# Attention in groups of four key slots, with one exponential over two PSUM banks

## The chip, the cores and the metric

The kernel runs on one core of one Trainium2 chip. The time is device microseconds of one launch, the median of several runs. Engines are named as in the profile: PE (TensorE matmuls), PEld (its weight loads), DVE (VectorE), ACT (ScalarE), POOL (GpSimd) and SP (SyncE, which issues all DMAs here).

## The reference

A block of three residual steps on x of shape (4, 1024, 128), in float32:

```python
x = x + 0.5 * ffn(layernorm(x))              # 8 experts, dense, weighted by a router
x = x + attn(layernorm(x))                   # attn has its own layernorm, and adds its input
x = x + 0.5 * ffn(layernorm(x))

# attn: 16 heads of 64, latents of 64
c_q, c_kv = h @ w_down_q.T, h @ w_down_kv.T
q, k, v = heads(c_q @ w_up_q.T), heads(c_kv @ w_up_k.T), heads(c_kv @ w_up_v.T)
q, k = rope(q), rope(k)
attn = softmax(q @ k.T / sqrt(64))           # no mask, 1024 keys
out = merge(attn @ v) @ w_out.T + residual
```

## The kernel before

The kernel has three stages one after another on all engines: the first feed-forward part (`ffn`), attention (the loop over `g` in `run`), the second feed-forward part (`ffn2`). The order of instructions on each engine is the order in which the program issues them; it is written by hand. The change is in attention.

**Units and slots.** Heads are taken in pairs `P` (32 of them: 4 batches by 8), queries in halves of 512. A pair and a half is a unit `U` (64 of them). In a unit, the 1024 keys are eight chunks of 128; one chunk is a slot `s` (512 in all). For a slot, `score` (L689) multiplies keys by queries for both heads of the pair (`hh`), in four accumulating steps `k`: three products of split high and low parts, and one that subtracts the row maximum (`one_row` by `maxr`). The two heads use the two row halves of the PE array side by side, tiling 64\*128 in the profile. An exponential (L705) turns the scores into `p`. POOL sums the `p` of slots 0 to 6 in `acc` (L717). `values` (L719) multiplies `p` by the latent (`psc`, L724; both heads beside each other by columns, 128\*64). After a unit, `den` (L728) sums `p` and `acc` over keys with ones, and the sum goes through DRAM to become a column `dT`; `outp` (L751) multiplies the unit's output by the folded matrix `G`, and DVE scales it by the reciprocal and adds it to `X` (L766).

**Maxima.** `passA` (L665) runs 15 slots ahead (`AHEAD`): one pair of matmuls into the two banks `psA`, and a DVE maximum over both (L677). `psA` is not doubled, so a pair must wait until the maximum before it has been taken. After eight of them `max_row` sends the maxima through DRAM to `maxr`.

**Other work.** `rope` makes the queries and keys of later heads, one tile per unit: matmuls `mm` (L595), four DVE products (L583), two POOL combinations `e` and `o`, ACT casts `hi0` and `hi1`, a POOL subtraction `lo`, and two DMAs `dhi` and `dlo`. The generators in `streams` (norms, latents, router of the second feed-forward part) advance by one stage at each `step`. `at(g, fn)` puts work off to a later group, `run_later` does it. `loads` brings queries and keys of a pair back from DRAM.

**Banks.** PSUM has eight banks: two `psA`, four `psS` for scores, `psC` for values, `psX`. A slot's scores take `psS[2 * (s % 2) + hh]`. Between scores, `psX` and `psS[0]` serve `rope` and `outp`, `psS[1]` and `psS[2]` the streams (`aux`), and `psX` the denominator.

**The cycle.** A group `g` is two slots:

```python
passA; scores of slot 2g; [rope e0, adds of outp, step]; scores of slot 2g+1; passA
rope (mm, ...); run_later (outp, ...); step; den; rope (casts, lo)
values of the two slots of the group before
```

Projection, output and denominator each come once in four groups, in different ones.

Of the kernel before, what the change touches and what calls it, by code (L numbers as in the profile page):

```python
# [9 lines left out]
F32 = mybir.dt.float32  # L10
# [16 lines left out]
AHEAD = 15  # L27
NSLOT = B * 128
NGRP = NSLOT // 2
# [8 lines left out]
class Kernel:  # L38
# [10 lines left out]
    def setup(self):  # L49
# [7 lines left out]
        bank = lambda name, n=1: pool(name, 1, space=PSUM).tile([128, 512] if n == 1 else [128, n, 512], F32, name=name)  # L57
        self.psA, self.psS, self.psC, self.psX = bank("ps_a", 2), [bank(f"ps_s{i}") for i in range(4)], bank("psc"), bank("psx")
# [40 lines left out]
        self.ckn = [const.tile([128, TPB, 64], F32, name=f"ckn{i}") for i in range(2)]  # L99

# [53 lines left out]
    def ffn_weights2(self, wg, wu, wd):  # L154
        self.wg, self.wu, self.wd = (w.rearrange("p k (e i) -> p k e i", e=E) for w in (wg, wu, wd))
        for n, w in enumerate((self.wg, self.wu)):
            self.dma(out=w, in_=self.w_scr[n])
        self.dma(out=self.wd[:, 1], in_=self.wd_scr)
        for n in range(4):
            es = bass.ds(2 * n, 2)  # L160
            hi, lo = self.wd[:, 0, es], self.wd[:, 1, es]
            self.at(self.group + 4 + n, lambda hi=hi, lo=lo: self.nc.scalar.copy(hi, self.f(lo)))
            self.at(self.group + 5 + n, lambda hi=hi, lo=lo: self.nc.gpsimd.tensor_tensor(lo, self.f(lo), self.f(hi), ALU.subtract))
# [407 lines left out]
    def rope(self, n, stage):  # L571


        nc, P = self.nc, self.prep
        w = self.rope_of.setdefault(n, {})
        b, m = divmod(n, 16)
        g, qk, h = m // 4, m // 2 % 2, m % 2
        scr = (self.k_scr if qk else self.q_scr)[b][g]
        cs = slice(512 * h, 512 * h + 512)

        def half(eo, k):
            w[eo, k] = P.tile([128, 512], F32, name=f"rt{eo}{k}", tag=f"t{2 * eo + k}")
            nc.vector.tensor_tensor(w[eo, k], w["ps"][eo], (self.cos, self.sin)[k][:, cs], ALU.mult)  # L583

        if stage == "fetch":
            assert (b, qk, h) in self.latents
            w["C"] = P.tile([128, 2, 512], F32R, name="C_l", bufs=2)
            self.dma(out=w["C"], in_=self.c_scr[b][h][:, qk])
        elif stage == "mm":
            ps = w["ps"] = self.rope_banks  # L590
            hi, lo = w["C"][:, 0, :], w["C"][:, 1, :]
            for k, (wt, c) in enumerate(((self.wup1, hi), (self.wup1, lo), (self.wup2, hi))):
                for eo in range(2):
                    r64 = slice(64 * eo, 64 * eo + 64)
                    nc.tensor.matmul(ps[eo], wt[r64, qk * 4 + g, :], c[r64, :], start=k == 0, stop=k == 2)  # L595
            half(1, 0)
            half(1, 1)
        elif stage in ("e0", "e1"):
            half(0, int(stage[1]))
        elif stage == "e":  # L600
            w["eo"] = P.tile([128, 2, 512], F32, name="eo", bufs=2)
            nc.gpsimd.tensor_tensor(w["eo"][:, 0, :], w[0, 0], w[1, 1], ALU.subtract)  # L602
        elif stage == "o":
            nc.gpsimd.tensor_tensor(w["eo"][:, 1, :], w[0, 1], w[1, 0], ALU.add)  # L604
        elif stage in ("hi0", "hi1"):
            k = int(stage[2])
            if k == 0:
                w["hi"] = P.tile([128, 2, 512], F32R, name="hi_r")
            nc.scalar.copy(w["hi"][:, k, :], w["eo"][:, k, :])  # L609
        elif stage == "dhi":  # L610
            self.dma(out=scr[0:2, :, :, cs].rearrange("s h i t -> (h i) s t"), in_=w["hi"])
        elif stage == "lo":
            nc.gpsimd.tensor_tensor(w["eo"].bitcast(F32R), w["eo"], self.f(w["hi"]), ALU.subtract)  # L613
        elif stage == "dlo":
            self.dma(out=scr[2:4, :, :, cs].rearrange("s h i t -> (h i) s t"), in_=w["eo"])
            self.roped.add((b, g, qk, h))
            del self.rope_of[n]

    def attn_first(self):

        yield from self.attn_pre(0)
        steps = {-5: "fetch", 0: "mm e0 e1", 2: "e", 3: "o", 5: "hi0", 6: "hi1", 7: "dhi", 8: "lo", 10: "dlo"}
# [33 lines left out]
    def at(self, g, fn):  # L656

        self.later.setdefault(g, []).append(fn)

    def run_later(self, g):  # L660
        self.group, self.slot = g, 2 * g
        for fn in self.later.pop(g, []):
            fn()

    def passA(self, a):  # L665
# [12 lines left out]
        if i == 7:  # L678
            m = self.ms.tile([128, 8], F32R, name="m8")
            nc.vector.tensor_reduce(m, self.m_of.pop(U).rearrange("p h q k -> p (h q) k"), AX.X, ALU.max, negate=True)  # L680
            self.at(self.group, lambda: self.max_row(U, m))

    def max_row(self, U, m):
# [3 lines left out]
        self.at(self.group + 2, lambda: self.dma(out=self.maxr[U % 2][0:128:64, :].rearrange("h (q p) -> h q p", p=128), in_=d.rearrange("p (h q) -> h q p", h=2)))  # L687

    def score(self, s, hh, k):  # L689
# [9 lines left out]
        ps = self.psS[2 * (s % 2) + hh]  # L699
        w, x = ((K[r, 0, ks], Q[r, 0, qs]), (K[r, 0, ks], Q[r, 1, qs]), (K[r, 1, ks], Q[r, 0, qs]), (self.one_row[r, :], self.maxr[U % 2][r, :]))[k]  # L700
        nc.tensor.matmul(ps, w, x, start=k == 0, stop=k == 3)  # L701
        if k == 3:
            if hh == 0:
                self.p_of[s] = self.pp.tile([128, 2, 512], F32, name="p")
            nc.scalar.activation(self.p_of[s][:, hh, :], ps, AF.Exp, scale=0.125)  # L705
            if hh == 1:
                self.accumulate(s)
# [20 lines left out]
    def den(self, U):  # L728
# [3 lines left out]
        pd = self.psX  # L732
# [10 lines left out]
        self.at(self.group + 1, lambda: nc.sync.dma_start(out=dT, in_=d1.rearrange("(h x) (y p) -> p (h x y)", x=2, p=128)))  # L743
        self.at(self.group + 2, lambda: self.invert(U, osb, dT))

    def invert(self, U, osb, dT):
        rT = self.ms.tile([128, 8], F32, name="rT")
        self.nc.vector.reciprocal(rT, dT)
        self.at(self.group + 1, lambda: self.outp(U, osb, rT))

    def outp(self, U, osb, rT):  # L751
# [11 lines left out]
        def add(hh):  # L763
            for i in range(4):
                x = self.X[:, b * TPB + 4 * half + i, :]
                nc.vector.scalar_tensor_tensor(x, po[hh][:, i * 128:(i + 1) * 128], rT[:, 4 * hh + i:4 * hh + i + 1], x, ALU.mult, ALU.add)  # L766

        add(1)
        if self.bankO:
            self.mid.append(lambda: add(0))  # L770
        else:
            add(0)

    def run(self):
# [21 lines left out]
        with ExitStack() as ctx:  # L796
# [20 lines left out]
            def bg1(n, point):  # L817
# [9 lines left out]
                if point == 2 and n >= 64 - AHEAD:  # L827
                    self.group = (n - 64) // 2
                    self.passA(n - 64 + AHEAD)
                    if n % 2:  # L830
                        self.run_later(self.group)
# [36 lines left out]
        self.rest, self.rope_banks, self.bankO = self.psS[1:3], [self.psX, self.psS[0]], [self.psX, self.psS[0]]  # L868
        self.mid = []
# [25 lines left out]
        MID, TAIL, END = {1: "e0"}, {3: "hi0 hi1 lo"}, {-2: "fetch", 0: "mm", 1: "e1", 2: "e o", 4: "dhi", 5: "dlo"}  # L895

        def rope(g, table):
            for d, stages in table.items():
                n, r = divmod(g - d - 1, 4)
                if r == 0 and 0 <= n + NROPE < 16 * B and n >= 0:  # L900
# [3 lines left out]
        rope(-1, {-2: "fetch"})  # L904
        for g in range(NGRP + 1):
            s0 = 2 * g
            self.group, self.slot = g, s0

            for s in range(s0, min(s0 + 2, NSLOT)):
                if s == s0 and s + AHEAD < NSLOT:  # L910
                    self.passA(s + AHEAD)
                for k in range(4):
                    for hh in range(2):
                        self.score(s, hh, k)
                if s == s0:
                    rope(g, MID)
                    if self.mid:
                        self.mid.pop()()
                    if g % 2:
                        step(False)  # L920
                elif s + AHEAD < NSLOT:
                    self.passA(s + AHEAD)

            while self.mid:
                self.mid.pop()()
            self.nrest = 0
# [3 lines left out]
            rope(g, END)  # L930
            self.run_later(g)
            if g % 4 != 1:
                step(g % 4 != 3)
            if g == 2:
                for n, fn in enumerate(self.loads(2)):
                    self.at(g + 1 + n // 4, fn)
            if g < NGRP and g % 8 == 7:
                P = g // 8
                if P + 3 < NP:
                    for n, fn in enumerate(self.loads(P + 3)):  # L940
                        self.at(g + 1 + n // 4, fn)
                if P == NP - 2:
# [3 lines left out]
            if g and g % 4 == 0:  # L946
                self.den(g // 4 - 1)
            rope(g, TAIL)
            for s in range(s0 - 2, s0):
# [9 lines left out]
        with ExitStack() as ctx:  # L959
            self.ready, self.routed = set(range(6)), set(range(6))  # L960
            assert not (streams[1] or streams[2])
# [5 lines left out]
            def bg2(n):  # L967
                self.run_later(NGRP + 1 + n)
# [5 lines left out]
            self.ffn2(x_of, bg2, self.out.rearrange("(n p) d -> p n d", p=128))  # L974
        att.close()
# [54 lines left out]
```

## Time and profile before

| | us |
|---|---|
| median of 3 runs | 1777.81 (1777.41 to 1781.66) |
| profiled execution | 1775.35 |
| its span | 1773.6 |
| PE busy | 1677.1 |
| POOL busy | 1462.2 |
| DVE busy | 1302.2 |
| ACT busy | 912.4 |

The profile is of one execution. A row of the groups gives line, engine, operation, tiles and shapes, count, busy time, mean ns of one, and the idle time of the engine just before with what ended it. The timeline gives start, length, engine, line and count. Weight loads overlap matmuls, and matmuls overlap each other: a pair of row-tiled matmuls of 512 columns has a length of 0.39 us in the timeline but the next pair starts 0.23 us later, so starts are read, not lengths. The idle time of an engine that does not set the end costs nothing.

### The profile page before, as it was taken

Reading aid. Unit: us, or ns where it says so; the run is one execution under the profiler, and the core shown is the slowest. Engines: PE = TensorE matmul, PEld = TensorE weight load, DVE = VectorE, ACT = ScalarE, POOL = GpSimd, SP = SyncE. Lnnn points to the kernel's source line nnn. Section 1 sums busy time; section 2 is a strip of 40 time slices with the busy share of each in tenths; the row PEclk is TensorE's granted clock in tenths of the full one; section 3 lists DMA queues with packets and bytes.
Section 4 is the critical chain, followed back from the end, with each engine's and each line's share of the span. In section 5 each row is a group of like instructions: output and inputs, shape, how many; then the busy total and the mean of one; then the engine's idle time right before and its main releaser. Section 6 shows DMA issues by size and latency. Waiting matters only on the chain.

```text
span 1773.6 us, 31244 instructions
## 1 busy us (share of the span) xinstructions
PE 1677.1 (95%) x11428; PEld 1006.7 (57%) x11428; DVE 1302.2 (73%) x2223; ACT 912.4 (51%) x1916; POOL 1462.2 (82%) x803
## 2 busy tenths in 40 slices
PE   6898989999899999999999999999999999999998
PEld 5777755555455555555555555555555555456777
DVE  6676658777877778777787777687677766834887
ACT  4666655545455454554544455544544544445554
POOL 4448779899899998998998899898999987667666
PEclk9999999999999999999999999999999999999999
DMA  6025455455444444455444544544455442023443
GB/s 200 1 72 181 132 147 147 134 143 139 113 135 139 135 136 116 120 144 144 131 121 123 140 122 129 135 121 120 132 135 139 120 99 61 2 86 110 140 124 103
DMA packets 241418, 216.00 MB, mean 122 GB/s; under 512 B 156785, under 2 KB 169713, under 8 KB 240625
## 3 DMA queue, kind: packets, MB, share of 16 engines
q1 hardware_dynamic: 241264, 214.01, 43.7%
q8 instruction: 90, 1.47, 0.4%
q14 instruction: 64, 0.52, 0.1%
HBM read 129.93 MB, written 84.02 MB: 121 GB/s over the span
## 4 chain that ended last, share of the span: by engine, by line
PE 71%; DVE 15%; ACT 5%; POOL 4%; issue 3%; DMA 1%; SPq 0%; DVEq 0%; ACTq 0%; POOLq 0%
PE psc L724 23%; PE ps_s L701 19%; PE ps_a L676 8%; DVE m L677 5%; PE psx L736 4%; PE ps_s L402 3%; DVE X L766 3%; ACT p L705 3%; PE ps_s L481 2%; PE psx L761 2%; PE psx L595 2%; PE psx L436 2%; PE psc L373 1%; POOL acc L717 1%; POOL p L489 1%
## 5 line engine op out<-in xcount | busy, mean ns | idle before, releaser
L677 DVE TENSOR_REDUCE m<-ps_a 128x2 f32<-128x1024 f32 x512 | 626.5, 1224 | 335.4 <-PE ps_a L676 334.7
L705 ACT ACTIVATE p<-ps_s 128x512 f32<-128x512 f32 x1024 | 530.4, 602 | 578.7 <-PE ps_s L701 559.8
L717 POOL TENSOR_TENSOR acc<-acc,p 128x1024 f32<-128x1024 f32 x320 | 761.3, 2379 | 66.8 <-ACT p L705 50.4
L724 PE MATMUL psc<-p,ckn 128*64 128x512 f32 x2048 | 496.6, 606 | 0.0
L701 PE MATMUL ps_s<-QT,KT 64*128 64x512 f32 x3072 | 445.8, 394 | 4.7 <-DVE X L766 3.1
L701 PEld LDWEIGHTS ps_s<-QT,KT 64*128 64x128 f32 x3072 | 290.7, 186 | 69.3 <-DVE X L766 6.7
L724 PEld LDWEIGHTS psc<-p,ckn 128*64 128x64 f32 x2048 | 124.3, 136 | 225.9 <-issue 214.6
L676 PE MATMUL ps_a<-KT,QT 64*128 64x512 f32 x1024 | 232.7, 449 | 17.6 <-DVE m L677 17.4
L676 PEld LDWEIGHTS ps_a<-KT,QT 64*128 64x128 f32 x1024 | 96.6, 184 | 238.4 <-DVE m L677 80.2
L717 POOL TENSOR_TENSOR acc<-p 128x1024 f32<-128x1024 f32 x64 | 151.6, 2369 | 72.2 <-ACT p L705 72.1
L701 PE MATMUL ps_s<-maxr,one_row 64*128 64x512 f32 x1024 | 204.7, 393 | 0.0
L613 POOL TENSOR_TENSOR eo<-eo,hi_r 128x1024 fp32r<-128x1024 f32 x64 | 153.3, 2396 | 20.9 <-ACT hi_r L609 20.9
L386 POOL TENSOR_TENSOR X<-X,dtmp 128x512 f32<-128x512 f32 x54 | 69.3, 1283 | 67.0 <-ACT dtmp L385 60.4
L701 PEld LDWEIGHTS ps_s<-maxr,one_row 64*128 64x128 f32 x1024 | 98.3, 186 | 22.0
L489 POOL TENSOR_TENSOR p<-eo,p 128x512 fp32r<-128x512 f32 x42 | 62.8, 1506 | 36.8 <-ACT p L488 34.2
L602 POOL TENSOR_TENSOR eo<-rt,rt 128x512 f32<-128x512 f32 x64 | 83.5, 1304 | 0.0
L604 POOL TENSOR_TENSOR eo<-rt,rt 128x512 f32<-128x512 f32 x64 | 82.4, 1288 | 0.0
L766 DVE SCALAR_TENSOR_TENSOR X<-ps_s,rT,X 128x128 f32<-128x128 f32 x252 | 70.3, 341 | 16.4 <-PE ps_s L761 16.3
L609 ACT CAST hi_r<-eo 128x512 fp32r<-128x512 f32 x128 | 73.9, 622 | 5.8 <-POOL eo L602 2.3
L402 PE MATMUL ps_s<-xs,wg 128*128 128x512 f32 x192 | 64.5, 445 | 10.5 <-DVE p L410 9.3
L766 DVE SCALAR_TENSOR_TENSOR X<-psx,rT,X 128x128 f32<-128x128 f32 x252 | 70.3, 341 | 0.0
L761 PEld LDWEIGHTS psx<-G,osb 64*128 64x128 f32 x504 | 65.5, 187 | 4.2
(195 smaller groups left out, 2193.9 us busy)
## 6 DMA issues: line engine op xcount, KB each, us to landing
C_l<-cs SPq DMA_DIRECT2D x64, 512.0 KB
QT<-qs SPq DMA_DIRECT2D x256, 128.0 KB
KT<-ks SPq DMA_DIRECT2D x256, 128.0 KB
qs<-hi_r SPq DMA_DIRECT2D x32, 512.0 KB
qs<-eo SPq DMA_DIRECT2D x32, 512.0 KB
ks<-hi_r SPq DMA_DIRECT2D x32, 512.0 KB
ks<-eo SPq DMA_DIRECT2D x32, 512.0 KB
wb<-wt SPq DMA_DIRECT2D x64, 256.0 KB
```

The costliest lines, as they stand in the source:

```text
L402: nc.tensor.matmul(p, w[:, a, e, :], xs[:, c, :], start=k == 0, stop=k == 2)
L602: nc.gpsimd.tensor_tensor(w["eo"][:, 0, :], w[0, 0], w[1, 1], ALU.subtract)
L604: nc.gpsimd.tensor_tensor(w["eo"][:, 1, :], w[0, 1], w[1, 0], ALU.add)
L613: nc.gpsimd.tensor_tensor(w["eo"].bitcast(F32R), w["eo"], self.f(w["hi"]), ALU.subtract)
L676: nc.tensor.matmul(self.psA[:, hh, :], self.QT[P % 3][r, 0, q0:q0 + 128], self.KT[P % 3][r, 0, kk * 512:kk * 512 + 512], start=True, stop= ...
L677: nc.vector.tensor_reduce(self.m_of[U][:, :, qb, kk], self.psA, AX.X, ALU.max)
L701: nc.tensor.matmul(ps, w, x, start=k == 0, stop=k == 3)
L705: nc.scalar.activation(self.p_of[s][:, hh, :], ps, AF.Exp, scale=0.125)
L717: nc.gpsimd.tensor_tensor(acc, self.p_of[s - 1] if c == 1 else acc, self.p_of[s], ALU.add)
L724: nc.tensor.matmul(self.psC[64 * hh:64 * hh + 64, :], self.ckn[b % 2][:, c, :], self.p_of[s][:, hh, :], start=c == 0, stop=c == 7)
L761: nc.tensor.matmul(po[hh][:, i * 128:(i + 1) * 128], osb[r, i * 128:(i + 1) * 128], self.G[r, j, :], start=True, stop=True)
L766: nc.vector.scalar_tensor_tensor(x, po[hh][:, i * 128:(i + 1) * 128], rT[:, 4 * hh + i:4 * hh + i + 1], x, ALU.mult, ALU.add)
```

## The change

A group is now four slots. The four score banks become two tiles of two banks, `psT[s % 2]`, and a slot's two heads are read by one exponential of 1024 columns in place of two of 512. In a group, PE runs the scores of four slots in a row. Maxima pairs stand before the scores, before the last step of the second slot (`n == 7`), before the third step of the fourth (`n == 14`), and after the side work. Put-off work has places in a group: `mid` (after `n == 7`), `side` (after the scores: rope `mm` in even groups, `outp` in odd ones), `end`; the casts of `rope` follow. Streams advance at `n == 7`, `n == 14` and once after the scores. `den` writes the second bank of `psT[0]`; `rope` and `outp` use `psX` and the first bank of `psT[0]`, the streams the second of `psT[1]`. The denominator's column is read back at `mid` of the next group, the output projected at its `side`, and the reciprocal and all eight additions come at its `end`. For the feed-forward parts the banks are set up as four single ones.

```diff
-NGRP = NSLOT // 2
+NGRP = NSLOT // 4
...
+    def four_banks(self):
+        self.banks = ExitStack()
+        self.psS = [self.bank(f"ps_s{i}", c=self.banks) for i in range(4)]
+
+    def two_pairs(self):
+        self.banks.close()
+        self.banks = ExitStack()
+        self.psT = [self.bank(f"ps_t{i}", 2, c=self.banks) for i in range(2)]
...
-    def run_later(self, g):
-        self.group, self.slot = g, 2 * g
-        for fn in self.later.pop(g, []):
+    def run_later(self, g, place):
+        self.group, self.slot = g, 4 * g
+        for fn in self.later.pop((g, place), []):
             fn()
...
-            self.at(self.group, lambda: self.max_row(U, m))
+            self.at(self.group, lambda: self.max_row(U, m), "mid")
...
-        ps = self.psS[2 * (s % 2) + hh]
+        ps = self.psT[s % 2][:, hh, :]
...
-        if k == 3:
-            if hh == 0:
-                self.p_of[s] = self.pp.tile([128, 2, 512], F32, name="p")
-            nc.scalar.activation(self.p_of[s][:, hh, :], ps, AF.Exp, scale=0.125)
-            if hh == 1:
-                self.accumulate(s)
+        if k == 3 and hh == 1:
+            self.p_of[s] = self.pp.tile([128, 2, 512], F32, name="p")
+            nc.scalar.activation(self.p_of[s], self.psT[s % 2], AF.Exp, scale=0.125)
+            self.accumulate(s)
...
-        pd = self.psX
+        pd = self.psT[0][:, 1, :]
...
-        self.at(self.group + 1, lambda: nc.sync.dma_start(out=dT, in_=d1.rearrange("(h x) (y p) -> p (h x y)", x=2, p=128)))
-        self.at(self.group + 2, lambda: self.invert(U, osb, dT))
+        last = U == 2 * 8 * B - 1
+        self.at(self.group + 1, lambda: nc.sync.dma_start(out=dT, in_=d1.rearrange("(h x) (y p) -> p (h x y)", x=2, p=128)), "mid")
+        self.at(self.group + (4 if last else 1), lambda: self.outp(U, osb, dT), "side")
...
+        self.at(self.group, add)
...
-        self.rest, self.rope_banks, self.bankO = self.psS[1:3], [self.psX, self.psS[0]], [self.psX, self.psS[0]]
+        self.two_pairs()
+        self.rest = [self.psT[1][:, 1, :]]
+        self.rope_banks = self.bankO = [self.psX, self.psT[0][:, 0, :]]
...
-        MID, TAIL, END = {1: "e0"}, {3: "hi0 hi1 lo"}, {-2: "fetch", 0: "mm", 1: "e1", 2: "e o", 4: "dhi", 5: "dlo"}
+        ROPE = {"mid": {2: "dhi"}, "side": {0: "mm"}, "end": {-1: "fetch", 0: "o0 o1 e0 e1 e o", 2: "dlo"}, "cast": {1: "hi0 hi1 lo"}}
...
         for g in range(NGRP + 1):
-            s0 = 2 * g
+            s0 = 4 * g
...
+            for n in range(16):
+                if n in (0, 7, 14):
+                    maxima(n // 7)
+                if g < NGRP:
+                    s, k = divmod(n, 4)
                     for hh in range(2):
-                        self.score(s, hh, k)
+                        self.score(s0 + s, hh, k)
+                if n == 7:
+                    rope(g, "mid")
+                    self.run_later(g, "mid")
+                if n in (7, 14):
+                    step(False)
+            rope(g, "side")
+            self.run_later(g, "side")
+            maxima(3)
...
+            step(True)
+            if g and g % 2 == 0:
+                self.den(g // 2 - 1)
+            rope(g, "end")
+            self.run_later(g, "end")
...
+            rope(g, "cast")
+            for s in range(s0 - 4, s0):
                 if s >= 0:
                     self.values(s)
```

More of the change, by code (lines that the diff above doesn't have):

```diff
@@ L55, in setup @@
         self.prep = pool("prep", 1)
-        bank = lambda name, n=1: pool(name, 1, space=PSUM).tile([128, 512] if n == 1 else [128, n, 512], F32, name=name)
-        self.psA, self.psS, self.psC, self.psX = bank("ps_a", 2), [bank(f"ps_s{i}") for i in range(4)], bank("psc"), bank("psx")
+        bank = lambda name, n=1, c=ctx: c.enter_context(tc.tile_pool(name=name, bufs=1, space=PSUM)).tile([128, 512] if n == 1 else [128, n, 512], F32, name=name)
+        self.bank = bank
+        self.psA, self.psC, self.psX = bank("ps_a", 2), bank("psc"), bank("psx")
+        self.four_banks()
         self.rest, self.nrest, self.slot, self.bankO = [self.psS[3]], 0, -NSLOT, None
@@ L161, in ffn_weights2 @@
             hi, lo = self.wd[:, 0, es], self.wd[:, 1, es]
-            self.at(self.group + 4 + n, lambda hi=hi, lo=lo: self.nc.scalar.copy(hi, self.f(lo)))
-            self.at(self.group + 5 + n, lambda hi=hi, lo=lo: self.nc.gpsimd.tensor_tensor(lo, self.f(lo), self.f(hi), ALU.subtract))
+            self.at(self.group + 2 + n // 2, lambda hi=hi, lo=lo: self.nc.scalar.copy(hi, self.f(lo)))
+            self.at(self.group + 2 + n // 2, lambda hi=hi, lo=lo: self.nc.gpsimd.tensor_tensor(lo, self.f(lo), self.f(hi), ALU.subtract))
     def attn_weights(self):
@@ L595, in rope @@
                     nc.tensor.matmul(ps[eo], wt[r64, qk * 4 + g, :], c[r64, :], start=k == 0, stop=k == 2)
[L596 to L599, printed above, removed]
+        elif stage in ("o0", "o1", "e0", "e1"):
+            half("eo".index(stage[0]), int(stage[1]))
         elif stage == "e":
@@ L621, in attn_first @@
         yield from self.attn_pre(0)
-        steps = {-5: "fetch", 0: "mm e0 e1", 2: "e", 3: "o", 5: "hi0", 6: "hi1", 7: "dhi", 8: "lo", 10: "dlo"}
+        steps = {-5: "fetch", 0: "mm o0 o1 e0 e1", 2: "e", 3: "o", 5: "hi0", 6: "hi1", 7: "dhi", 8: "lo", 10: "dlo"}
         for t in range(-5, 6 * (NROPE - 1) + 11):
@@ L654, in load, with at @@
             fn()
-    def at(self, g, fn):
-        self.later.setdefault(g, []).append(fn)
-    def run_later(self, g):
-        self.group, self.slot = g, 2 * g
-        for fn in self.later.pop(g, []):
+    def at(self, g, fn, place="end"):
+        self.later.setdefault((g, place), []).append(fn)
+    def run_later(self, g, place):
+        self.group, self.slot = g, 4 * g
+        for fn in self.later.pop((g, place), []):
             fn()
@@ L686, in max_row @@
         self.dma(out=d, in_=m)
-        self.at(self.group + 2, lambda: self.dma(out=self.maxr[U % 2][0:128:64, :].rearrange("h (q p) -> h q p", p=128), in_=d.rearrange("p (h q) -> h q p", h=2)))
+        self.at(self.group, lambda: self.dma(out=self.maxr[U % 2][0:128:64, :].rearrange("h (q p) -> h q p", p=128), in_=d.rearrange("p (h q) -> h q p", h=2)))
     def score(self, s, hh, k):
@@ L742, in den, with outp @@
         nc.sync.dma_start(out=d1, in_=dsb[0:128:32, :])
-        self.at(self.group + 1, lambda: nc.sync.dma_start(out=dT, in_=d1.rearrange("(h x) (y p) -> p (h x y)", x=2, p=128)))
-        self.at(self.group + 2, lambda: self.invert(U, osb, dT))
[L746 to L751, printed above, removed]
+        last = U == 2 * 8 * B - 1
+        self.at(self.group + 1, lambda: nc.sync.dma_start(out=dT, in_=d1.rearrange("(h x) (y p) -> p (h x y)", x=2, p=128)), "mid")
+        self.at(self.group + (4 if last else 1), lambda: self.outp(U, osb, dT), "side")
+    def outp(self, U, osb, dT):
         nc = self.nc
@@ L761, in outp, with add @@
                 nc.tensor.matmul(po[hh][:, i * 128:(i + 1) * 128], osb[r, i * 128:(i + 1) * 128], self.G[r, j, :], start=True, stop=True)
[L763 to L772, printed above, removed]
+        def add():
+            rT = self.ms.tile([128, 8], F32, name="rT")
+            nc.vector.reciprocal(rT, dT)
+            for hh in (1, 0):
+                for i in range(4):
+                    x = self.X[:, b * TPB + 4 * half + i, :]
+                    nc.vector.scalar_tensor_tensor(x, po[hh][:, i * 128:(i + 1) * 128], rT[:, 4 * hh + i:4 * hh + i + 1], x, ALU.mult, ALU.add)
+        self.at(self.group, add)
     def run(self):
@@ L827, in bg1 @@
                 if point == 2 and n >= 64 - AHEAD:
-                    self.group = (n - 64) // 2
+                    self.group = (n - 64) // 4
                     self.passA(n - 64 + AHEAD)
-                    if n % 2:
-                        self.run_later(self.group)
+                    if n % 4 in (1, 3):
+                        self.run_later(self.group, ("mid", "end")[n % 4 // 2])
                 if point < 3:
@@ L867, in run @@
         assert not (streams[0] or streams[2])
-        self.rest, self.rope_banks, self.bankO = self.psS[1:3], [self.psX, self.psS[0]], [self.psX, self.psS[0]]
-        self.mid = []
+        self.two_pairs()
+        self.rest = [self.psT[1][:, 1, :]]
+        self.rope_banks = self.bankO = [self.psX, self.psT[0][:, 0, :]]
         streams[2] += [self.attn_pre(b) for b in range(1, B)]
@@ L892, in step, with rope @@
                     return
-        MID, TAIL, END = {1: "e0"}, {3: "hi0 hi1 lo"}, {-2: "fetch", 0: "mm", 1: "e1", 2: "e o", 4: "dhi", 5: "dlo"}
[L897 to L900, printed above, removed]
+        ROPE = {"mid": {2: "dhi"}, "side": {0: "mm"}, "end": {-1: "fetch", 0: "o0 o1 e0 e1 e o", 2: "dlo"}, "cast": {1: "hi0 hi1 lo"}}
+        def rope(g, place):
+            for d, stages in ROPE[place].items():
+                n, r = divmod(g - d, 2)
+                if r == 0 and 0 <= n and n + NROPE < 16 * B:
                     for stage in stages.split():
                         self.rope(n + NROPE, stage)
-        rope(-1, {-2: "fetch"})
+        rope(-1, "end")
         for g in range(NGRP + 1):
-            s0 = 2 * g
+            s0 = 4 * g
             self.group, self.slot = g, s0
[L909 to L912, printed above, removed]
-                    for hh in range(2):
-                        self.score(s, hh, k)
[L915 to L926, printed above, removed]
+            maxima = lambda i: self.passA(s0 + AHEAD + i) if s0 + AHEAD + i < NSLOT else None
+            for n in range(16):
[3 more added lines that the diff above has]
+                    s, k = divmod(n, 4)
+                    for hh in range(2):
+                        self.score(s0 + s, hh, k)
[7 more added lines that the diff above has]
+            maxima(3)
             b, i = divmod(s0, 128)
@@ L929, in run @@
                 streams[1].append(pre2(b - 1))
[L930 to L942, printed above, removed]
+            step(True)
[3 more added lines that the diff above has]
+            self.run_later(g, "end")
+            if g == 1 or (g < NGRP and g % 4 == 3):
+                P = g // 4 + 3 if g > 1 else 2
+                if P < NP:
+                    for n, fn in enumerate(self.loads(P)):
+                        self.at(g + 1 + n // 8, fn, ("mid", "end")[n // 4 % 2])
+                if P == NP + 1:
                     self.ffn_weights2(self.QT[a], self.KT[a], self.QT[c])
                     self.dma(out=xs[0], in_=self.x2_scr[0])
[L946 to L949, printed above, removed]
+            rope(g, "cast")
+            for s in range(s0 - 4, s0):
                 if s >= 0:
@@ L960, in run @@
             self.ready, self.routed = set(range(6)), set(range(6))
+            self.banks.close()
+            self.four_banks()
             assert not (streams[1] or streams[2])
@@ L967, in bg2 @@
             def bg2(n):
-                self.run_later(NGRP + 1 + n)
+                for place in ("mid", "side", "end"):
+                    self.run_later(NGRP + 1 + n, place)
                 if n >= GS:
@@ L974, in run @@
             self.ffn2(x_of, bg2, self.out.rearrange("(n p) d -> p n d", p=128))
+        self.banks.close()
         att.close()
```

## The prediction

> **What bounds the kernel now.** I read the page first: engine shares, chain, groups. Then the attention stage alone by windows (the first PV matmul is at 244 us, the last at 1614 us), then PE's waits in that window, then one cycle in the timeline.
>
> ```profile
> span 1773.6 us, 31244 instructions
> PE 1677.1 (95%) x11428; PEld 1006.7 (57%) x11428; DVE 1302.2 (73%) x2223; ACT 912.4 (51%) x1916; POOL 1462.2 (82%) x803
> PE 71%; DVE 15%; ACT 5%; POOL 4%; issue 3%; DMA 1%; SPq 0%; DVEq 0%; ACTq 0%; POOLq 0%
> L705 ACT ACTIVATE p<-ps_s 128x512 f32<-128x512 f32 x1024 | 530.4, 602 | 578.7 <-PE ps_s L701 559.8
> ```
> PE sets the end. The exponentials (L705) leave ACT idle 578.7 us, nearly all waiting for scores: ACT is not short of time.
>
> ```profile
> 244.00:1614.00 1370.00, 1323.33 (x9599) 724.84 (x9599) 1004.61 (x1618) 683.46 (x1365) 1208.71 (x590) 1.00 0.45 120
> PE psx L736 <- DVE X L766: 16.8, 33, 0.7
> PE ps_a L676 <- DVE m L677: 15.0, 18, 2.0
> ```
> The first row is the stage by windows: length, then busy PE, PEld, DVE, ACT, POOL, then clock, DMA share, GB/s. PE is busy 1323 of 1370 us; POOL's 1209 is a floor 160 us below. PE's own waits are small; the largest is the denominator (L736), whose bank psx still holds output sums that DVE reads.
>
> The timeline shows a cycle of two slots without side matmuls:
> ```profile
> 856.80 0.50 PE L676 MATMUL ps_a<-KT,QT 64*128 64x512 f32 x2
> 857.14 0.85 PE L701 MATMUL ps_s<-QT,KT 64*128 64x512 f32 x6
> 857.83 0.39 PE L701 MATMUL ps_s<-maxr,one_row 64*128 64x512 f32 x2
> 859.00 0.40 PE L676 MATMUL ps_a<-KT,QT 64*128 64x512 f32 x2
> 859.32 1.94 PE L724 MATMUL psc<-p,ckn 128*64 128x512 f32 x8
> 859.44 1.23 DVE L677 TENSOR_REDUCE m<-ps_a 128x2 f32<-128x1024 f32 x1 [0.27 <-PE ps_a L676]
> 860.23 0.14 PEld L724 LDWEIGHTS psc<-p,ckn 128*64 128x64 f32 x2 [0.28 <-issue]
> 861.19 0.50 PE L676 MATMUL ps_a<-KT,QT 64*128 64x512 f32 x2
> ```
> Start to start the cycle is 4.39: maxima pair to scores 0.34 (0.11 more than the usual 0.23 of a pair: its weights are loaded in the open after the change from 128*64 to 64*128), two slots of scores 1.86, second maxima pair to values 0.32 (0.09 more), values 1.87 (first pair 0.48, three at 0.43, 0.10 until the next kind). So one round trip between the two tilings costs about 0.11 + 0.09 + 0.15 = 0.35.
>
> How a wait is paid shows where the rope projection needed a bank that an exponential held:
> ```profile
> 722.25 2.06 ACT L705 ACTIVATE p<-ps_s 128x512 f32<-128x512 f32 x4
> 722.90 0.18 PEld L595 LDWEIGHTS ps_s<-C_l,wup 64*128 64x128 f32 x1 [1.00 <-ACT p L705]
> 722.90 0.50 PE L595 MATMUL ps_s<-C_l,wup 64*128 64x512 f32 x1 [0.57 <-ACT p L705]
> 723.25 0.39 PE L595 MATMUL ps_s<-C_l,wup 64*128 64x512 f32 x1
> ```
> The bank is free at 722.25 + 0.60; PE restarts 0.05 later, and the next pair follows after 0.35 instead of 0.23: a wait costs its length plus 0.11. Four exponentials take 2.06, so they follow each other every 0.49 when none waits.
>
> **The change part by part.** I count in units of eight slots (64 of them): before four cycles, after two. Before, from timeline rows: plain 4.39, with rope projection 5.08 (806.74 to 811.82), with output projection 5.27 (840.35 to 845.62), with denominator 5.93 (823.82 to 829.75) of which about 0.5 is the wait above, so 5.40 without. Sum 20.14; the 33 waits add (16.8 + 33 x 0.11)/64 = 0.32: 20.46. The measured unit is 1370/64 = 21.4; the rest is matmuls of the norm and router streams (some 0.5) and irregular lateness, which I carry over unchanged.
>
> *Fewer tiling changes.* Two round trips fewer per unit: 2 x 0.35 = 0.70, 45 us in all.
>
> *The denominator's bank* is now one that an exponential freed earlier, and the adds come behind it: -0.32 per unit, 20 us.
>
> *The score burst.* Four slots in a row on two pairs of banks: slot 2 needs the exponential of slot 0, slot 3 that of slot 1. Before, values stood between reuses and no score waited for ACT. No row has 1024 columns. Copies on ACT take 370 (256 columns) and 587 ns (512), 0.85 ns a column, so 602 + 512 x 0.85 = 1.03 us. Bounds: 1.01 (the 0.80 of the final copies) and 1.09 (0.60 + 0.49). From the first maxima pair at 0: slot 0 at 0.34, its last pair at 1.03; an exponential starts about 0.49 after the last pair (807.78 to 808.27): 1.52 to 2.55. Slot 1 from 1.27 with the second maxima inside, last pair 2.20, exponential 2.69 to 3.72. Slot 2 wants 2.43 and gets 2.60. Slot 3 gets 3.77; without waits it had started at 3.36. So 0.41 plus 0.11 reload: 0.52 per cycle, 1.04 per unit, 67 us.
>
> *The third and fourth maxima.* The third pair stands after slot 3's second step: 3.77 + 0.34 + 0.23 = 4.34. DVE reads it 0.44 later (859.00 to 859.44) for 1.23, PE may go on 0.06 after: 6.07. In between PE has slot 3's rest (to 5.04) and one side job, 0.69 (rope) or 0.88 (output): it is done at 5.73 or 5.92 and waits 0.34 or 0.15, plus 0.11 reload. Per unit 0.71, 45 us.
>
> *Sum.* Fourth maxima 6.07, values from 6.50, four slots of values 0.48 + 7 x 0.43 + 0.10 = 3.59: the odd cycle takes 10.09, the even one with the denominator's 1.01 takes 11.10. A unit is 21.19 against 20.46: +0.73 x 64 = +47 us. By terms: -45 - 20 + 67 + 45 = +47. If no wait costs a reload and the exponential takes 1.01, the unit is 20.71: +16.
>
> *Merging two exponentials* moves a slot's end on ACT from 1.09 (two, 0.60 + 0.49) to 1.03 (one), which the schedule above contains. Beyond that the saved ACT time is worth nothing: ACT idles 578.7 us. The Trainium skill, "Perfetto Trace Analysis", Optimizing Scalar/DVE Operations, speaks against it: engines that are not saturated but cause bubbles elsewhere should have their instructions broken up so that work completes sooner. By that, two halves would free the first bank at +0.60; but the pairs of a slot alternate between its two banks, and the second would be free at 1.09. I take nothing either way; by the rule alone the 67 us would be the merge's fault and an unmerged burst would gain.
>
> *A second rule against it.* Small gaps after PE bursts that cycle through PSUM banks make the clock gate fall back ("TensorE: Matmul & The Clock Gate", A second HAM failure mode). Here the granted clock of the stage is 1.00 with waits of 0.7 and 1.0 us in it, and after the wait at 722.90 matmuls take 0.39 as elsewhere. By the row: nothing. By the rule, even a quarter of each burst of some 5 us at half rate would be 1.2 x 128 = 160 us slower. I go by the row.
>
> *Side work moved.* POOL has the same instructions: per unit 6 additions x 2.38, rope 1.30 + 1.29 + 2.40: 19.3 of 21.2; they were late by up to a few us before and their readers (denominator in the next unit's first cycle, p buffers eight slots on) leave 6 us. DVE: rope halves (4 in some 2.5 after the fourth maxima at 7.8, done 10.3 of 11.1) and reciprocal plus eight additions (0.19 + 2 x 1.11, done 10.2 of 10.1, the next maxima read at 10.6): covered, with 0.4 left in the odd cycle; a stream step longer than that delays the second maxima. ACT: the casts stand behind the last exponential, 4 us before the next. SP: loads eight per cycle in two places as often per slot as before; the dT read has half a cycle (some 4 us) and dhi, dlo, the maxima's row a cycle or more, against issues of 0.4 to 0.5 us. Cost nothing while so covered; a late dT would hold DVE, and the next maxima with it (before: 14.6 us in three waits). Nothing else is queued behind a new SP wait for longer than the denominator's copy, 1 to 2 us. Setting up the banks anew happens twice: under 1 us.
>
> **The rivals.** *Faster: the burst does not wait.* Then a bare cycle is 0.34 + 4 x 0.93 + 2 x 0.23 + 0.32 + 3.59 = 8.43, a unit (8.43 + 0.69 + 1.01) + (8.43 + 0.88) = 19.44, 1.02 less: -65 us, 1713. The sum breaks even where each cycle loses 0.36 less, an exponential of 0.67. For it: no score ever waited for ACT before, and POOL's floor (1209/64 = 18.9 a unit) allows it. Against: 0.60 for half the width. Chance 0.15.
>
> *Much slower: side work in the burst.* Stream steps now stand behind slot 1 and inside slot 3; their ACT instructions (norms) can wait for DVE (L227 in the window: 13.3 + 14.3 + 11.8 = 39 us before), and hold the next exponential. Two slots had 2.5 us of slack, the burst has none; if all of it lands on PE: +47 + 39, 1864. Chance 0.11.
>
> *Cheaper waits.* If loads are pulled ahead and terms cancel, +16 or less, 1773 to 1793, no change within reach. A swap of tiles that does nothing is excluded: the order of PE's work is changed in every cycle. Chance 0.12, of which half within 0.3%.
>
> *Main case*, 1793 to 1850: chance 0.62.
>
> **How the numbers follow.** The profiled execution took 1775.35 us (span 1773.6), 2.5 below the median 1777.81. 1775.35 + 47 + 2.5 = 1824.9; the streams' share of lateness with the denominator wait gone is worth a few us less, so 1822. The range takes in the cheaper waits and most of the side-work case, 1778 to 1860; it leaves out the faster case and the far end. 0.3% is 5 us, about what runs of this kernel can tell from no change: faster 0.16, same 0.06, slower 0.78.
>
> **What would show it.** Right: L701's matmuls wait for ACT some 0.2 to 0.4 us in each cycle, where it was never named before; L676 waits for DVE m in most cycles; L705 has 512 instructions of about 1.03 us; L736 no longer waits for DVE X; values come in runs of 16 matmuls, 128 times; cycles of about 10.1 and 11.1. Wrong: cycles near 9.3 and 10.1, exponentials near 0.7, a clock below 0.97 in the stage, or PE waiting for POOL.

## The result: 4% slower

The changed kernel takes 1850.8 us (median of 4 runs, 1847.87 to 1854.35) against 1778.85 for the kernel before: ratio 1.0402, 95% interval 1.0384 to 1.042, so 72 us more. The forecast was 1822, in the range 1778 to 1860, with a main case that ended at 1850: the sign and the waits of the sum are right, but 25 us of the 72 are not in it (it came to 47).

The page of the changed kernel, same parts as before:

```profile
span 1846.1 us, 30620 instructions
PE 1724.1 (93%) x11428; PEld 1012.5 (55%) x11428; DVE 1296.9 (70%) x2223; ACT 905.2 (49%) x1404; POOL 1462.6 (79%) x803
PE 59%; DVE 17%; SPq 7%; DMA 5%; ACT 5%; issue 3%; POOL 3%; POOLq 0%; ACTq 0%; DVEq 0%
L716 ACT ACTIVATE p<-ps_t 128x1024 f32<-128x1024 f32 x512 | 520.8, 1026 | 447.3 <-PE ps_t L713 425.7
```

ACT's busy time is nearly unchanged although it has 512 instructions fewer: busy time counts once where two short exponentials overlapped (1024 of 602 ns would have been 616 us; the row before had 530.4). One merged exponential takes 1026 ns; 1.03 had been worked out. New is SPq with 7% and DMA with 5% of the chain that ended last. In the kernel before they had 0% and 1%.

The waits of PE and its weight loads (in total us, times, longest) in the attention stage, 244 to 1690 us, and the largest DMA wait of DVE in the whole span:

```profile
PE ps_a L688 <- DVE m L689: 29.4, 82, 2.2
PE ps_t L713 <- DVE X L775: 16.7, 21, 1.8
PE ps_t L713 <- ACT p L716: 10.4, 42, 0.3
PEld ps_t L713 <- ACT p L716: 102.5, 221, 0.7
DVE rT L771 <- DMA dT<-d: 59.2, 26, 11.4
```

Scores (L713) now wait for ACT, which they never did. The wait shows mainly in the row of the weight loads, 102.5 us in 221 places: the matmul before is still running when its load begins to wait. The reciprocal of the denominator (L771) waits 59.2 us for its column from DRAM, four times the 14.6 us of the kernel before.

One even cycle in the timeline (start, length), to be read against the schedule of the prediction:

```profile
886.04 0.50 PE L688 MATMUL ps_a<-KT,QT 64*128 64x512 f32 x2
887.32 0.86 PE L713 MATMUL ps_t<-QT,KT 64*128 64x512 f32 x6
888.60 0.96 PE L713 MATMUL ps_t<-QT,KT 64*128 64x512 f32 x6
889.77 0.73 PE L713 MATMUL ps_t<-QT,KT 64*128 64x512 f32 x4
890.35 0.39 PE L688 MATMUL ps_a<-KT,QT 64*128 64x512 f32 x2
892.06 0.50 PE L688 MATMUL ps_a<-KT,QT 64*128 64x512 f32 x2 [0.15 <-DVE m L689]
893.49 3.65 PE L734 MATMUL psc<-p,ckn 128*64 128x512 f32 x16
897.07 0.50 PE L688 MATMUL ps_a<-KT,QT 64*128 64x512 f32 x2
```

From the first row on: slot 1 at 1.28, slot 2 at 2.56 (worked out 2.60), slot 3 at 3.73 (3.77), third maxima at 4.31 (4.34), fourth at 6.02 (6.07), values at 7.45 (6.50 + 1.01), next cycle at 11.03 (11.10).

### The profile page after: what moved, and what is told of

It reads as the page before. It is cut to its first block, busy times and chain, and to the rows that moved or that the text cites. A ratio compares the mean times of both kernels' runs of the same rounds, so it can differ in the third digit from the quotient of the medians.

```text
span 1846.1 us, 30620 instructions
## 1 busy us (share of the span) xinstructions
PE 1724.1 (93%) x11428; PEld 1012.5 (55%) x11428; DVE 1296.9 (70%) x2223; ACT 905.2 (49%) x1404; POOL 1462.6 (79%) x803
## 4 chain that ended last, share of the span: by engine, by line
PE 59%; DVE 17%; SPq 7%; DMA 5%; ACT 5%; issue 3%; POOL 3%; POOLq 0%; ACTq 0%; DVEq 0%
PE psc L734 18%; PE ps_t L713 15%; DVE m L689 8%; PE ps_a L688 8%; SPq L47 7%; PE ps_s L415 3%; PE ps_t L746 3%; ACT p L716 3%; PE ps_s L494 3%; DVE X L775 3%; DMA dT<-d 2%; DMA C_l<-cs 2%; PE psx L449 2%; PE psc L386 1%; POOL acc L727 1%
## 5 line engine op out<-in xcount | busy, mean ns | idle before, releaser
L716 ACT ACTIVATE p<-ps_t 128x1024 f32<-128x1024 f32 x512 | 520.8, 1026 | 447.3 <-PE ps_t L713 425.7
L713 PE MATMUL ps_t<-QT,KT 64*128 64x512 f32 x3072 | 487.1, 408 | 31.8 <-DVE X L775 16.7
L734 PE MATMUL psc<-p,ckn 128*64 128x512 f32 x2048 | 469.3, 600 | 0.0
L713 PEld LDWEIGHTS ps_t<-QT,KT 64*128 64x128 f32 x3072 | 270.7, 185 | 174.6 <-ACT p L716 104.5
L734 PEld LDWEIGHTS psc<-p,ckn 128*64 128x64 f32 x2048 | 136.1, 137 | 264.0 <-issue 263.2
L713 PE MATMUL ps_t<-maxr,one_row 64*128 64x512 f32 x1024 | 203.0, 391 | 0.0
L736 ACT COPY osb<-psc 128x512 f32<-128x512 f32 x64 | 37.6, 588 | 189.4 <-PE psc L734 189.4
L713 PEld LDWEIGHTS ps_t<-maxr,one_row 64*128 64x128 f32 x1024 | 97.2, 185 | 17.0
L775 DVE SCALAR_TENSOR_TENSOR X<-ps_t,rT,X 128x128 f32<-128x128 f32 x252 | 71.1, 344 | 12.5 <-PE ps_t L767 4.9
```

Source lines behind the costliest of these rows:

```text
L716: nc.scalar.activation(self.p_of[s], self.psT[s % 2], AF.Exp, scale=0.125)
L734: nc.tensor.matmul(self.psC[64 * hh:64 * hh + 64, :], self.ckn[b % 2][:, c, :], self.p_of[s][:, hh, :], start=c == 0, stop=c == 7)
```

## The experiments

Cycle lengths below are from one start of a run of values to the next, in the trace of each kernel; "regular" is the median of the cycles without a matmul of the streams, or their lower quartile where more than half of them are late. The changed kernel has 10.08 (odd, output projection) and 11.07 (even, rope and denominator, lower quartile; the median is 11.52). Differences in us between kernels are worked out from the ratios to the kernel before, taken at 1778 us.

**Third maxima pair earlier.** Changed kernel with

```diff
-                if n in (0, 7, 14):
-                    maxima(n // 7)
+                if n in (0, 7, 12):
+                    maxima((0, 7, 12).index(n))
```

> The third maxima pair stands between slot 2 and slot 3 instead of inside slot 3; nothing else changes. Theory (the waits of the burst and of the fourth maxima set the cycle): the pair falls into the time in which slot 3 waits for its exponential, its maximum is done at 5.5 after the cycle's start, and the fourth pair follows the side job at 5.66 or 5.85 instead of 6.07. A unit of eight slots goes from 21.19 to 20.34: 54 us faster than the changed kernel, some 1797 us. PE waits on DVE m almost vanish. Rival (late side work, above all the denominator's column from DRAM, is what costs): within 10 us of the changed kernel, 1841 to 1861.

Measured: 1819.1 us, ratio 1.0257 (1.0234 to 1.028), 26 us faster than the changed kernel. The pair fills slot 3's wait, and the fourth follows the side job at once (rows of its timeline):

```profile
1003.35 0.50 PE L688 MATMUL ps_a<-KT,QT 64*128 64x512 f32 x2
1007.23 0.50 PE L688 MATMUL ps_a<-KT,QT 64*128 64x512 f32 x2
1007.57 0.86 PE L713 MATMUL ps_t<-QT,KT 64*128 64x512 f32 x6
1008.97 0.40 PE L608 MATMUL psx<-C_l,wup 64*128 64x512 f32 x1
1009.19 0.41 PE L688 MATMUL ps_a<-KT,QT 64*128 64x512 f32 x2
```

The fastest even cycle takes 10.57 (10.58 was worked out), their lower quartile 10.68; odd ones 9.89 (9.76), since the output projection then waits for slot 2's exponential, whose bank it takes. (11.07 - 10.68 + 10.08 - 9.89) x 64 = 37 us of the 54 are in the regular cycles; some 11 of them came back as lateness. The weight loads' wait of the scores for ACT falls from 102 to 40 us. The waits on DVE's maxima did not vanish, against the expectation: PE's own are 28.6 us as against 27.2. DVE still waits 57.9 us for the column, but that is only a part of it: with the column read early as well ("Both moves" below) 20.6 us are left. Half the size, but the mechanism as described.

**Two exponentials, first form.** Changed kernel, an exponential of 512 after each head's last step, on the same two-bank tiles:

```diff
-        if k == 3 and hh == 1:
-            self.p_of[s] = self.pp.tile([128, 2, 512], F32, name="p")
-            nc.scalar.activation(self.p_of[s], self.psT[s % 2], AF.Exp, scale=0.125)
-            self.accumulate(s)
+        if k == 3:
+            if hh == 0:
+                self.p_of[s] = self.pp.tile([128, 2, 512], F32, name="p")
+            nc.scalar.activation(self.p_of[s][:, hh, :], ps, AF.Exp, scale=0.125)
+            if hh == 1:
+                self.accumulate(s)
```

> Groups of four as in the changed kernel, but each slot's two banks are read by two exponentials of 512 columns, as before. Theory (the grouping makes the wait, not the merge): the second bank of a slot is free at 0.60 + 0.49 = 1.09 instead of 1.03, so 0.06 more in each of 128 cycles: 8 us slower, 1850 to 1862. Rival [...]: the first bank is free 0.43 earlier, the burst's wait goes, up to 67 us faster, 1784 to 1810.

Measured: 2410.1 us, ratio 1.3534 (1.3456 to 1.3612). Neither theory. The waits (first row) and the timeline show another edit than the one meant:

```profile
PE ps_t L713 <- ACT p L717: 429.7, 512, 4.4
```

```profile
1007.12 0.39 PE L713 MATMUL ps_t<-maxr,one_row 64*128 64x512 f32 x1
1007.60 0.60 ACT L717 ACTIVATE p<-ps_t 128x512 f32<-128x512 f32 x1 [5.08 <-PE ps_t L713]
1008.25 0.50 PE L713 MATMUL ps_t<-maxr,one_row 64*128 64x512 f32 x1 [0.74 <-ACT p L717]
```

Once in every slot (512 times) the second head's last matmul waits for the first head's exponential, though it writes the other bank: the two banks are one tile, and the program orders a write to the tile behind a read issued before it. The pair of heads is torn apart. The run says nothing on the merge, and it shows that on these tiles a bank is not free before all that was issued earlier on the tile has been read.

**Two exponentials behind the pair.** The same question, both exponentials issued after the slot's last matmul:

```diff
-            nc.scalar.activation(self.p_of[s], self.psT[s % 2], AF.Exp, scale=0.125)
+            for i in range(2):
+                nc.scalar.activation(self.p_of[s][:, i, :], self.psT[s % 2][:, i, :], AF.Exp, scale=0.125)
```

> The changed kernel with two exponentials of 512 columns for a slot, both behind the slot's last matmul, on the same two-bank tiles. Theory (grouping makes the wait): a slot is free at 1.09 instead of 1.03, 0.06 in each of 128 cycles: 8 us slower than the changed kernel, 1850 to 1862. Rival (a merged instruction is what holds PE): faster by tens of us.

Measured: 1853.77 us, ratio 1.0428 (1.0407 to 1.0449), 5 us slower than the changed kernel, with intervals that overlap. Regular cycles are 10.14 and 11.14, 0.06 and 0.07 longer, as worked out. In groups of four on these tiles the merge is worth about nothing, and does no harm. Since the tile's two banks come free together here (the run before), a split on four single banks, whose first would be free earlier, is not tested; that the pair would then wait for its second bank is argued only.

**The merge alone.** Kernel before, with the pair tiles, their setting up, and the merged exponential of the changed kernel; groups of two as before:

```diff
-        ps = self.psS[2 * (s % 2) + hh]
+        ps = self.psT[s % 2][:, hh, :]
...
+            nc.scalar.activation(self.p_of[s], self.psT[s % 2], AF.Exp, scale=0.125)
...
+        self.rest = [self.psT[0][:, 1, :], self.psT[1][:, 0, :]]
+        self.rope_banks = self.bankO = [self.psX, self.psT[0][:, 0, :]]
```

> The kernel before with only the merge: a slot's two banks as one tile, one exponential of 1024 columns; groups of two slots as before. Theory: scores never wait, but the rope and output projections take the bank of slot 0's first head 2.43 after the cycle's start; it was free at 2.17 and is free at 2.60 now. 116 waits of 0.17 and a reload of 0.11: some 32 us slower, ratio 1.012 to 1.024. Rival (ACT time saved is worth something, or the exponential's end does not matter): ratio 0.99 to 1.003.

Measured: 1797.16 us, ratio 1.0112 (1.0094 to 1.0131), 20 us slower. The rope cycle goes from 5.08 to 5.37, the output cycle from 5.28 to 5.56: 0.28 each, as worked out. 116 of them are 32 us and only 20 arrived; 10 us came back in the 64 cycles with a denominator, which last 397 us together as against 407 in the kernel before. The row of the weight loads names the wait, 53 of the 55 rope projections:

```profile
PEld ps_t L608 <- ACT p L717: 20.0, 53, 1.3
```

So the rule that the prediction weighed (the Trainium skill, "Perfetto Trace Analysis", Optimizing Scalar/DVE Operations: breaking up instructions of an engine that is not saturated but makes bubbles elsewhere may let work complete sooner) holds here, by 0.28 a cycle, where somebody waits for the first bank. Where the next user needs both, the 0.06 of the run before shows nothing to gain from it, on tiles whose banks come free together.

**Values split.** Changed kernel, two of the four values moved between slots 1 and 2:

```diff
                 if n == 7:
+                    for s in range(s0 - 4, s0 - 2):
+                        if s >= 0:
+                            self.values(s)
...
-            for s in range(s0 - 4, s0):
+            for s in range(s0 - 2, s0):
```

> Groups of four, but two of the four values of the group before stand between slot 1 and slot 2, two at the end. Theory: the burst's wait goes (-1.04 per unit), the two tiling round trips come back (+0.70), the fourth maxima still wait: a unit takes 20.87 instead of 21.19, 20 us faster than the changed kernel, some 1830 us, and PE no longer waits for L716. Rival (scores waiting for ACT lie beside another wait and cost nothing by themselves): only the round trips are added, 45 us slower, some 1895.

Measured: 1954.25 us, ratio 1.1037 (1.0979 to 1.1096), 113 us slower than the changed kernel. Both theories miss. The half cycle from the middle values to the end values is as scheduled: 5.56 (odd) and 6.51 (even), worked out as 5.54 and 6.55. The other half should take 4.39 and has a median of 5.55: 1.16 in each of 127, 147 us. PE's waits say why:

```profile
PE ps_t L713 <- DVE X L775: 53.8, 52, 3.3
PE ps_a L688 <- DVE m L689: 43.7, 115, 1.3
PE ps_t L713 <- DVE rt L596: 25.3, 14, 3.5
```

The additions and the rope products read psT[0], and the next group's first scores need it. Four slots of values (3.59) cover that work; two (1.87) do not. PE's own wait of the scores for ACT falls from 10.4 to 1.4 us, as the schedule said, and a larger one came where the cover was taken away. The granted clock is also lower, 0.969 to 0.98 in the four runs as against 0.985 to 0.989; its share of the 147 us was not separated.

**Column read early.** Changed kernel, `dT` read in the group that wrote it:

```diff
-        self.at(self.group + 1, lambda: nc.sync.dma_start(out=dT, ...), "mid")
+        self.at(self.group, lambda: nc.sync.dma_start(out=dT, ...), "end")
```

> The denominator's column dT is read back from DRAM right at the end of the group that wrote it, instead of at mid of the next one behind that group's loads. Theory: DVE's wait for it (59.2 us in 26 times in the changed kernel) falls below 15 us; the additions come in time, the first scores of the next group no longer wait for them (16.7 us on PE and its reloads), and the even cycles lose part of their lateness: 20 us faster (10 to 30), 1820 to 1840. Rival (DVE had time, the lateness comes from router and norm steps): under 5 us. Second rival: SP now waits for the write to land in front of the loads, and maxima or loads come late: slower.

Measured: 1822.62 us, ratio 1.0269 (1.025 to 1.0288), 24 us faster. The waits, same rows as in the changed kernel:

```profile
DVE rT L771 <- DMA dT<-d: 22.3, 2, 11.4
PE ps_t L713 <- DVE X L775: 4.6, 7, 0.8
```

Of the column's 26 waits 2 are left, and the even cycles' median falls from 11.52 to 11.08, their regular length. The cause is in SP's queue. In half the units of the changed kernel the read is issued behind four loads of the group (SP's timeline: start, length until the next can issue):

```profile
937.48 0.54 SPq L752 DMA_DIRECT2D d<-dsb  x1
940.93 0.55 SPq L47 DMA_DIRECT2D maxr<-d  x1
941.52 5.39 SPq L47 DMA_DIRECT2D QT<-qs  x4
946.95 0.42 SPq L754 DMA_DIRECT2D dT<-d  x1
```

It goes out 9.5 us after the write that it reads. Of the 30 readings behind loads DVE waited for 24; of the 32 directly behind the row of maxima (`maxr`), for one. The four loads take 5.4 us, but 4.0 of these are the first one's, and they are not the load's own doing: the issue directly behind `maxr` is long whatever it is. In another unit of the changed kernel it is the column itself, and in the kernel before (the last two rows) a load of latents:

```profile
1231.86 0.54 SPq L47 DMA_DIRECT2D maxr<-d  x1
1232.50 3.86 SPq L754 DMA_DIRECT2D dT<-d  x1
699.74 0.53 SPq L47 DMA_DIRECT2D maxr<-d  x1
700.33 3.95 SPq L47 DMA_DIRECT2D C_l<-cs  x1
```

Between 262 and 1590 us all 59 issues behind `maxr` take 2.8 to 4.4 us in the changed kernel, and no other takes more than 2.5. What in the transfer of `maxr` holds the queue, no run shows. In the kernel before the column went out ahead of `maxr` (the order in its SP timeline); a line that the diff above passes over turned that round:

```diff
-        self.at(self.group + 2, lambda: self.dma(out=self.maxr...
+        self.at(self.group, lambda: self.dma(out=self.maxr...
```

The early read is still behind `maxr` in 62 of 64 units, but ahead of the loads, and that is early enough. A read ahead of `maxr` was not tried.

**Both moves.** The earlier pair and the early column together (the two diffs above).

> The third maxima pair between slots 2 and 3, and the denominator's column read back early, together. Theory: the two causes are separate. The regular cycles lose the 0.44 (even) and 0.19 (odd) that the earlier pair alone already showed, 40 us in all, and the early column takes its 28 us: some 68 to 80 us below the changed kernel, 1770 to 1783, level with the kernel before. Rival (both hide the same wait of PE): no better than the better of the two, 1805 to 1820.

Measured: 1797.55 us, ratio 1.0108 (1.009 to 1.0126), 52 us faster than the changed kernel. Alone they gave 26 and 24: they add, so the causes are separate. Both sizes were expected too large, so the version is not level with the kernel before but 19 us above it. Its regular unit is 10.68 + 9.89 = 20.57, nearly that of the kernel before (20.51, see below): only some 4 of the 19 us are in the regular cycles, the others are irregular lateness and the start of the stage, and stay open.

**Maxima evenly.** Both moves, and the second pair one step earlier:

```diff
-                if n in (0, 7, 12):
-                    maxima((0, 7, 12).index(n))
+                if n in (0, 6, 12):
+                    maxima(n // 6)
```

> Both moves of the changed kernel (column read early, third pair between slots 2 and 3), and the second pair one step earlier, inside slot 1. Theory: maxima pairs cannot follow each other faster than 1.73 (0.44 + 1.23 + 0.06); at 0, 1.73 and 3.64 the third no longer waits for the second's maximum, slot 3 starts at 3.87 instead of 4.04: 0.17 in each of 128 cycles, 22 us below the run with both moves, 1770 to 1785, level with the kernel before. Rival (with no slack left between the first two maxima, every late addition of DVE now stops PE one step earlier): no gain, 1795 to 1805.

Measured: 1799.38 us, ratio 1.012 (1.0102 to 1.0137): no gain. The regular cycles stay at 10.68 and 9.89. The first pair of a cycle loads its weights in the open, so its maximum starts 0.54 and not 0.44 after it: the second pair goes out at 1.83 at the earliest, has to reload, and slot 1's exponential starts later by what slot 3 was to gain.

**The denominator's bank.** In the kernel before, the denominator in `psS[1]`, the streams first in `psS[2]`:

```diff
-        pd = self.psX
+        pd = self.psS[1]
...
-        self.rest, ... = self.psS[1:3], ...
+        self.rest, ... = [self.psS[2], self.psS[1]], ...
```

> The kernel before, with the denominator in the bank of slot 0's second head instead of psx (and the streams taking the other bank first). Theory: the denominator no longer waits for DVE's additions from psx, 33 waits of 0.5 us and their reloads: 20 us faster than before, ratio 0.987 to 0.991. Rival (the maxima that DVE owes to the next cycle are late anyway, so the wait comes back there): ratio 0.997 to 1.003.

Measured: ratio 1.0001 (0.9991 to 1.0011). The cycle with the denominator goes from 5.93 to 5.53, but one with a latent projection of the streams as well goes from 6.58 to 7.06: the streams now take a bank whose exponential ends later, and a wait stands among PE's that was not there. The rival got the number right for another reason than it gave:

```profile
PE ps_s L546 <- ACT p L705: 6.6, 12, 0.6
```

**The denominator's bank where it is free.** Kernel before, one line:

```diff
-        pd = self.psX
+        pd = self.psX if self.nrest else self.psS[1]
```

> The kernel before; the denominator takes the bank of slot 0's second head in cycles in which no stream stage used it, psx in the others; nothing else changes. Theory: in the cycles without a stream matmul (38 of 64) the denominator's cycle goes from 5.93 to 5.53 as in the run with the other bank throughout, and the streams keep their bank, so their 0.48 does not come back: 38 x 0.40 = 15 us, ratio 0.989 to 0.994, below both kernels. Rival (PE is held by what comes behind, DVE's maxima, and any gain is lost to it): ratio 0.997 to 1.003.

Measured: 1763.14 us, ratio 0.991 (0.9895 to 0.9924): 16 us faster than the kernel before, and below both kernels. The denominator's cycle is 5.53, that with a latent projection 6.58 as before, and the 33 waits of the denominator for DVE's additions are gone from the trace. This sizes the term of the sum, and is a gain of the changed kernel that was had without the rest.

## Why the prediction was right, and where its size was not

*Fewer tiling changes (-45).* Right in the trace: values run in 16 matmuls and take 3.58 (893.49 to 897.07; 3.59 worked out). No experiment took this term alone.

*The denominator's bank (-20).* Right in kind, somewhat too large: 16 us where the same was done in the kernel before. Its cycle without the wait is 5.53 and not 5.40, so the wait is 0.40 in 38 of 64 cycles, and the unit before comes to 4.39 + 5.08 + 5.27 + 5.53 + 38 x 0.40 / 64 = 20.51 instead of 20.46.

*The burst (+67) and the fourth maxima (+45).* Right: every start in the cycle is met within 0.07, and moving one pair shortens the cycle where the schedule says. The regular unit is 10.08 + 11.07 = 21.15 (21.19 in the prediction) against 20.51: 41 us of the 72.

*"Side work moved ... cost nothing while so covered."* Here the sum failed. The reading of `dT` was costed at nothing with "half a cycle (some 4 us)" to spare, with SP's issues at 0.4 to 0.5 us. The trace of the kernel before already had an issue of 3.95 us behind `maxr`; it did no harm, for the column had gone out ahead of it. In the changed kernel the column stands behind it, in 30 of 64 units behind four loads as well: in these the read is out 9.8 us after the write (median), in those without loads 5.7. It came late in 26 units, and by the early read that costs 24 us. The rival of side work had looked for such a loss on ACT; it was on SP and DVE. That 1850.8 still lies in the range is in part luck: it is just above the main case, in the part of the range that was kept for ACT.

*The rest,* 72 - 41 - 24 = 7 us, was not tried alone. Nine units have no rope projection. In the kernel before that saved 0.70 each (5.08 against 4.38), in the changed one nothing (11.05 to 11.08 where nothing is late), because the fourth maxima pair waits for DVE anyway: some 5 us in the seven of them that still have maxima. The stage also starts at a lower clock (0.74 against 0.91 granted between 240 and 260 us).

*The two rules weighed.* Breaking up the exponential makes a cycle 0.06 longer: the trace's reading held on these tiles. The clock did not fall back: 0.989 over the changed kernel, 1.00 between 260 and 1600 us, with waits of 0.1 to 0.4 in every cycle.

*"What would show it"* named scores waiting for ACT, exponentials of 1.03, cycles of 10.1 and 11.1 and no wait of the denominator on DVE: all four are in the trace.

## What to carry to other kernels

Before work is grouped to save switches on PE, follow one buffer round: the time from the last matmul of a slot over its exponential to the bank's release must fit between two uses, here 1.03 + 0.54 = 1.57 against 0.93 + 0.23 = 1.16 for slot 3, and the work between uses was what had hidden it. Values and the like have a second task as cover for what other engines do on shared banks; moved away, they leave that work in the open. A small DMA with a deadline belongs in front of bulk loads in its queue; and before a queue is taken as free, read the length of every kind of issue in it, not the usual one: here one transfer held the next issue for 4 us.

## What the runs showed of the hardware that was not expected

A transfer of 4 KB can hold the queue behind it: the issue that follows `maxr` took some 4 us whatever it moved, others on SP mostly 0.4 to 0.8. The trace does not say why.

In the run with the torn pair the clock was lower too: each slot waited 0.84 us on average for an exponential (429.7 us in 512 waits), PE was busy 80% of the span, and the granted clock was 0.905 to 0.926 in the four runs, against 93% and 0.985 to 0.989 in the changed kernel with its shorter waits. That is the side of the clock gate which the second rule describes (the Trainium skill, "TensorE: Matmul & The Clock Gate", A second HAM failure mode); whether the length of the gaps or the share of busy time brings it on was not tried.
